# A four-layer hybrid network on one core: layer 0's last convolution, output and attention products arranged anew

## The chip, the cores and the metric

The kernel runs on one core of a Trainium2 chip. The metric is the time of the whole program on the device, in microseconds (us). Engines are named as in the profile: PE (TensorE, matrix products), DVE (VectorE), ACT (ScalarE), POOL (GpSimd), SP (SyncE, which here only issues transfers). Each engine works its own queue in order.

## The reference, cut to what matters

The input is 4 images of 256 channels and 32 x 32 pixels, all in fp32. Four layers follow; the change is in layer 0, a Mamba2 block with a channel attention, and touches the start of layers 1 and 2.

```python
u = layernorm(x over channels) * norm_g + norm_b          # 4 images of 1024 tokens, 256 channels
z, xBC, dt = split(u @ in_w.T)                            # 256, 512, 4 columns
dt = softplus(dt + dt_bias)
xBC = silu(conv1d(xBC, conv_w, 4 taps, causal, per channel) + conv_b)
xs, Bm, Cm = split(xBC)                                   # 256 (4 heads of 64), 128, 128
for t:                                                    # a recurrence over the 1024 tokens
    state = state * exp(dt[t] * A) + dt[t] * xs[t] * Bm[t]
    y[t] = state @ Cm[t]
y = (y + Dp * xs) * silu(z)
y = y * rsqrt(mean(y * y) + 1e-5) * rms_w
out = y @ out_w.T
hdn = relu(mean_over_tokens(out) @ se1_w.T + se1_b)
x = x + out * sigmoid(hdn @ se2_w.T + se2_b)              # one factor per image and channel
```

Layer 1 projects x by three vectors (theta, phi, g), forms one number per token from them, normalises it over all tokens and adds it back, scaled per channel. Layer 2 is softmax attention (Wq, Wk, Wv) and a mixture of 8 experts; layer 3 is an attention over channels and an LSTM over the 1024 tokens.

## The kernel before

The program is written in a tile language: the author issues operations and names tiles, pools give out buffers, and a scheduler at build time decides each engine's order, with semaphores where data or buffers demand a wait. It may move an instruction far ahead of where it is written, unless the code keeps it (`keep_in_program_order`, `issue_after`, `manual_schedule`). On the chip each order is fixed.

**Setup and `_project`** (lines 168 to 314). Weights come by ACT's queue (L177 `w_l0`, L179 `se2`, L181 `wide`: five rows of 256 broadcast to 128 partitions), x by SP's (L239). The tokens go in 8 blocks of 512, two to an image. `load` turns x by PE (L244; the same product gives theta, phi and g of x), ACT copies the rows (L247), DVE copies `of_x` (L248) and takes statistics, POOL makes the reciprocal root, DVE normalises (`un`, L156). `turn` transposes back, `project` makes z, dt (L274) and xBC (L282). After an image's second block `convolve` (L287) makes for each of 4 channel groups one ACT pass (L292), three DVE passes over 1024 columns (L297) and an ACT Silu (L300). After the last block `_decays` (L317) turns all dt into the recurrence's factors, by ACT exp and ln, DVE, and three PE products (L353). The scheduler has put at the head of DVE the scaling of `w_out` by `rms_w` (L199) and that of the LSTM's bias row (L1423), and at the head of ACT the exp of `A_log` (`na`, L347).

**`_scan`** (L359) does the recurrence in 8 tiles of 128 tokens per image. A tile: three transposes and one product on PE (L373, L374); ACT copies `xb` (L376) and makes `au` (L384); PE `pd` (L386), ACT exp (L388), DVE times the mask (`m_h`, L389); three POOL products (`xdt` L392, `y` L398, `xw` L401); PE `py` (L395) and the state's products (L404, L409); on DVE the sums of y (L399, L406, L407), the state (L411, L412) and the gate `zs` (L415); ACT squares (L417).

**`_out`** (L420), once per image: POOL reciprocal roots (L429, L430), DVE diagonals (L437), 16 PE products that scale and turn (L441), ACT copies with sums (`yT`, L445), the pooled sum (L450), its product with `w_out` (L454), mean (L459), product with `w_se1` (L462), ACT relu (`hdn`, L464), product with `se2` (L466), DVE add (`att`, L468), ACT tanh (L469), DVE half (L470), DVE `w_att` = `w_out` times att (L472), six DVE passes that multiply it by theta, phi and g and sum (L476). Then 8 tiles: PE products (L484), DVE adds to `rows` (L487), ACT copy of the three projections (`of_y`, L488). The order as written is recurrence of image b, then output of image b-1; output of the last two images comes after the last recurrence.

**`_layer1`** (L491) is a short chain of DVE and PE on one number per token, ending in `l1_row` (L553). **`_layer2_attention`** (L556) loads `w_l2`, multiplies Wq by Wk (`m_qk`, L590; `b_qk`, L596, L600), and works image by image from there. The LSTM's weights are loaded and scaled (L1415 to L1424) beside the experts of layer 2.

Of the kernel before, what the change touches and what calls it, by code (L numbers as in the profile page):

```python
# [13 lines left out]
ALU = mybir.AluOpType  # L14
# [44 lines left out]
    "norm_g": 2, "norm_b": 2, "conv_w": 16, "conv_b": 4, "rms_w": 2, "se1_b": 1,  # L59
# [64 lines left out]
def _weights(s, name):  # L124
    w = s.wpool.tile([P, C, NW[name]], F32, name=name, tag="w")
    s.nc.scalar.dma_start(w, s.d[name].rearrange("(k p) n -> p k n", p=P))
    return w
# [40 lines left out]
def _layer0_and_1(s):  # L168
# [5 lines left out]
    with ExitStack() as ctx:  # L174
# [5 lines left out]
        wide = keep.tile([P, 5, D], F32, name="wide")  # L180
        nc.scalar.dma_start(  # L181
            wide.rearrange("p i d -> p (i d)"), s.d["wide"].to_broadcast([P, 5 * D])
# [4 lines left out]
            three=wide[:, 2:, :],  # L187
# [10 lines left out]
        for k in range(C):  # L198
            nc.vector.tensor_scalar_mul(  # L199
                v.w_out[:, k, :], v.w_out[:, k, :], s.col["rms_w"][:, k : k + 1]  # L200
            )
        _project(s, v, keep)
        v.dt, v.decay, v.total, v.tail = v.decays
        with ExitStack() as body:
            pools = SimpleNamespace(
                scan=body.enter_context(tc.tile_pool(name="ssm", bufs=2)),
                out=body.enter_context(tc.tile_pool(name="out", bufs=2)),
                ps=body.enter_context(tc.tile_pool(name="ssm_ps", bufs=2, space=PSUM)),
            )
            for b in range(B):  # L210
                _scan(s, v, pools, b)
                if b > 0:
                    _out(s, v, pools, b - 1)
            _out(s, v, pools, B - 1)
# [3 lines left out]
def _project(s, v, keep):  # L218
# [4 lines left out]
    with ExitStack() as ctx:  # L223
# [5 lines left out]
        for k in range(C):  # L229
            nc.vector.tensor_copy(turner[:, k, 3:], s.ident)  # L230
            for j, name in enumerate(("theta_w", "phi_w", "g_w")):
                nc.vector.tensor_copy(turner[:, k, j : j + 1], s.col[name][:, k : k + 1])
        held = {}
# [53 lines left out]
        def convolve(b):  # L287
            for m in range(NXBC):
                x = v.xbc[b][:, m, :]
                acc = pool.tile([P, L], F32, name="acc")  # L290
                tap = s.col["conv_w"][:, m * DCONV : (m + 1) * DCONV]
                nc.scalar.activation(  # L292
                    acc, x[:, off:], AF.Identity,
                    bias=s.col["conv_b"][:, m : m + 1], scale=tap[:, off:],
                )
                for j in range(off):
                    nc.vector.scalar_tensor_tensor(  # L297
                        acc, x[:, j : j + L], tap[:, j : j + 1], acc, ALU.mult, ALU.add
                    )
                nc.scalar.activation(x[:, off:], acc, AF.Silu)  # L300
# [4 lines left out]
        for i in range(NBLK):  # L305
# [7 lines left out]
            if i % BPI == BPI - 1:  # L313
                convolve(i // BPI)


def _decays(s, keep, pool, ps, dtr):  # L317
# [29 lines left out]
    nc.scalar.activation(na, s.row["A_log"], AF.Exp)  # L347
# [11 lines left out]
def _scan(s, v, pools, b):  # L359


    nc, pool, ps = s.nc, pools.scan, pools.ps
    (a, head), xbc, zs = v.decay, v.xbc[b], v.zs[b]
    off = DCONV - 1
    state = pool.tile([P, NH, HD], F32, name="state")
    for c in range(TPI):
        n = b * TPI + c
        t = slice(off + c * P, off + (c + 1) * P)
        bT, cT = xbc[:, 2, t], xbc[:, 3, t]

        ptr = ps.tile([P, 4, P], F32, name="ptr")
        for m in range(3):
            nc.tensor.transpose(ptr[:, m, :], xbc[:, m, t], s.ident)  # L373
        nc.tensor.matmul(ptr[:, 3, :], bT, cT, start=True, stop=True)  # L374
        xb = pool.tile([P, 3, P], F32, name="xb")
        nc.scalar.copy(xb, ptr[:, :3, :])  # L376
        gm = pool.tile([P, P], F32, name="gm")
        nc.vector.tensor_mul(gm, ptr[:, 3, :], s.upper)
        xh = xb[:, :2, :].rearrange("p c (h d) -> p (c h) d", d=HD)


        au = pool.tile([P, NH, P], F32, name="au")
        for h in range(NH):
            nc.scalar.mul(au[:, h, :], s.upper, a[:, n, h : h + 1])  # L384
        pd = ps.tile([P, NH, P], F32, name="pd", bufs=1)
        nc.tensor.matmul(pd, s.lower, au, start=True, stop=True)  # L386
        m_h = pool.tile([P, NH, P], F32, name="m_h")
        nc.scalar.activation(m_h, pd, AF.Exp)  # L388
        nc.vector.tensor_mul(m_h, m_h, _bc(gm, 1, NH))  # L389

        xdt = pool.tile([P, NH, HD], F32, name="xdt")
        nc.gpsimd.tensor_mul(xdt, xh, _bc(v.dt[:, n, :], 2, HD))  # L392
        py = ps.tile([P, NH, HD], F32, name="py", bufs=1)
        for h in range(NH):
            nc.tensor.matmul(py[:, h, :], m_h[:, h, :], xdt[:, h, :], start=True, stop=True)  # L395

        y = pool.tile([P, NH, HD], F32, name="y")
        nc.gpsimd.tensor_mul(y, xh, _bc(s.row["Dp"], 2, HD))  # L398
        nc.vector.tensor_add(y, y, py)  # L399
        xw = pool.tile([P, NH, HD], F32, name="xw")  # L400
        nc.gpsimd.tensor_mul(xw, xh, _bc(v.tail[:, n, :], 2, HD))  # L401
        pst = ps.tile([P, 2, NH, HD], F32, name="pst")
        if c > 0:
            nc.tensor.matmul(pst[:, 0], cT, state, start=True, stop=True)  # L404
            y_in = pool.tile([P, NH, HD], F32, name="y_in")
            nc.vector.tensor_mul(y_in, pst[:, 0], _bc(head[:, n, :], 2, HD))  # L406
            nc.vector.tensor_add(y, y, y_in)  # L407
        if c < TPI - 1:
            nc.tensor.matmul(pst[:, 1], xb[:, 2, :], xw, start=True, stop=True)  # L409
            if c > 0:  # L410
                nc.vector.tensor_mul(state, state, _bc(v.total[:, n, :], 2, HD))  # L411
                nc.vector.tensor_add(state, state, pst[:, 1])  # L412
            else:
                nc.vector.tensor_copy(state, pst[:, 1])
        nc.vector.tensor_mul(zs[:, c, :], zs[:, c, :], y.rearrange("p h d -> p (h d)"))  # L415
        sq = pool.tile([P, D], F32, name="sq")
        nc.scalar.activation(sq, zs[:, c, :], AF.Square, accum_out=v.ss[:, n : n + 1])  # L417


def _out(s, v, pools, b):  # L420


    nc, pool, ps = s.nc, pools.out, pools.ps

# [6 lines left out]
    yT = pool.tile([P, C, L], F32, name="yT", bufs=1)  # L431
# [19 lines left out]
    p = small(P, C)  # L451
    for m in range(C):
        for k in range(C):
            nc.tensor.matmul(  # L454
                p[:, m : m + 1], v.w_out[:, k, bass.ts(m, P)], pooled[:, k : k + 1],
                start=k == 0, stop=k == C - 1,
            )
    mean = pool.tile([P, C], F32, name="mean")
    nc.vector.tensor_scalar_mul(mean, p, 1.0 / L)  # L459
    p = small(NSE, 1)  # L460
    for k in range(C):
        nc.tensor.matmul(p, v.w_se1[:, k, :], mean[:, k : k + 1], start=k == 0, stop=k == C - 1)  # L462
    hdn = pool.tile([NSE, P], F32, name="hdn")
    nc.scalar.activation(hdn, p.to_broadcast([NSE, P]), AF.Relu, bias=s.col["se1_b"][:NSE])  # L464
    p = small(P, D)
    nc.tensor.matmul(p, hdn, v.se2, start=True, stop=True)  # L466
    att = pool.tile([P, D], F32, name="att")
    nc.vector.tensor_add(att, p, v.se2_b)  # L468
    nc.scalar.activation(att, att, AF.Tanh, scale=0.5)  # L469
    nc.vector.tensor_scalar(att, att, 0.5, 0.5, ALU.mult, ALU.add)  # L470
    w = pool.tile([P, C, D + 3], F32, name="w_att")
    nc.vector.tensor_mul(w[:, :, :D], v.w_out, _bc(att, 1, C))  # L472
    for k in range(C):
        for j in range(3):
            junk = pool.tile([P, D], F32, name="junk")
            nc.vector.scalar_tensor_tensor(  # L476
                junk, w[:, k, :D], 1.0, v.three[:, j, :], ALU.mult, ALU.mult,
                accum_out=w[:, k, D + j : D + j + 1],
            )
    for j in range(TPI):  # L480
        n = b * TPI + j
        p = small(P, D + 3)
        for k in range(C):
            nc.tensor.matmul(  # L484
                p, yT[:, k, bass.ts(j, P)], w[:, k, :], start=k == 0, stop=k == C - 1
            )
        nc.vector.tensor_add(s.rows[:, n, :], s.rows[:, n, :], p[:, :D])  # L487
        nc.scalar.copy(v.of_y[:, n, :], p[:, D:])  # L488
# [67 lines left out]
def _layer2_attention(s):  # L556
# [6 lines left out]
    w = _weights(s, "w_l2")  # L563
    wq, wk, wv = (w[:, :, j * D : (j + 1) * D] for j in range(3))
    w_gate = w[:, :, 768:776]
# [5 lines left out]
    with ExitStack() as ctx:  # L571
        keep = ctx.enter_context(tc.tile_pool(name="l2_keep", bufs=1))
# [11 lines left out]

        m_qk = keep.tile([P, C, D], F32, name="m_qk")
        b_qk = keep.tile([P, C], F32, name="b_qk")
        for m in range(C):
            p = slim()
            for k in range(C):
                nc.tensor.matmul(  # L590
# [1240 lines left out]
```

## Time and profile before

| | |
|---|---|
| five runs, median (lowest to highest) | 3439.68 us (3438.15 to 3443.64) |
| the profiled execution: its time, its span | 3440.76 us, 3439.1 us |
| busy: PE, DVE, ACT, POOL | 3119.0, 1840.3, 1099.0, 533.9 us |
| mean granted TensorE clock | 0.986 |
| projection, decays, last convolution | 0 to 150 us |
| recurrence (first `xb` to last square) | 150.15 to 295.5 us |
| output of images 2 and 3 alone | to 337.3 us |
| layer 1 (`l1_row` ready) | to 344.5 us |
| layers 2 and 3 | to 3439.1 us |

Over 3000 of the 3439 us lie in layers 2 and 3, whose code the change leaves as it is but for the moved lines named above. In the profile "busy" is the time in which an engine works; a bracket behind an operation says how long its engine stood idle before it and which operation ended that. Idle time matters only where nothing else sets the pace.

### The profile page before, as it was taken

How to read it: one execution, taken by the hardware profiler on the slowest of the kernel's cores; microseconds unless marked ns; L12 is line 12 of the kernel's file. 1: busy time of each engine (PE TensorE's matmuls, PEld its weight loads, DVE VectorE, ACT ScalarE, POOL GpSimd, SP SyncE). 2: the span in 40 equal slices, each digit the busy share in tenths (PEclk: the TensorE clock that was granted, in tenths of full speed). 3: DMA queues.
4: the chain of work that ended last, by engine and by line, in shares of the span. 5: the costliest groups of instructions: out<-in, count | busy, mean ns of one | idle time of the engine just before them, and what ended most of it. 6: DMA issues, size and time to landing. Idle time of an engine off the chain costs nothing.

```text
span 3439.1 us, 143780 instructions
## 1 busy us (share of the span) xinstructions
PE 3119.0 (91%) x63650; PEld 2503.2 (73%) x63650; DVE 1840.3 (54%) x8205; ACT 1099.0 (32%) x4339; POOL 533.9 (16%) x749
## 2 busy tenths in 40 slices
PE   8797999999999989998998998998998998998887
PEld 5475577688888856777777777777777777777776
DVE  5786644651111144565655565555655665655555
ACT  5763222222222222333332332332332332332222
POOL 2252100124444320001001001001001001001000
PEclk9898899999999999999999999999999999999999
DMA  2000011256666620000000000000000000000000
GB/s 82 1 1 10 1 43 38 102 170 194 193 193 193 189 62 1 4 4 10 4 4 9 4 4 9 5 4 8 6 4 8 6 4 8 6 4 8 6 4 10
DMA packets 49459, 138.94 MB, mean 40 GB/s; under 512 B 4992, under 2 KB 38336, under 8 KB 44224
## 3 DMA queue, kind: packets, MB, share of 16 engines
q0 software_dynamic: 19008, 99.32, 9.3%
q1 hardware_dynamic: 27680, 24.45, 2.2%
q8 instruction: 499, 8.18, 0.9%
q10 hardware_dynamic: 2144, 5.95, 0.5%
q14 instruction: 128, 1.05, 0.1%
HBM read 104.21 MB, written 25.49 MB: 38 GB/s over the span
## 4 chain that ended last, share of the span: by engine, by line
PE 28%; DVE 20%; ACT 10%; issue 5%; DMA 1%; ACTq 0%; POOL 0%; DVEq 0%; SPq 0%
PE pre L1657 16%; DVE col L1668 11%; PE pre L1600 6%; ACT tri L1671 5%; DVE scan L1680 5%; DVE hs L1691 4%; PE p_a L1554 3%; PE p_d L1258 1%; PE p_k L1226 1%; DMA acc<-y,late_rows 1%; ACTq L1671 0%; PE p_d L1266 0%; PE p_w L1246 0%; PE p_w L165 0%; PE p_u L1388 0%
## 5 line engine op out<-in xcount | busy, mean ns | idle before, releaser
L1657 PE MATMUL pre<-w_v,hs 128*4 128x64 f32 x49104 | 872.9, 219 | 210.2 <-DVE hs L1691 199.1
L1657 PEld LDWEIGHTS pre<-w_v,hs 128*4 128x4 f32 x49104 | 684.1, 86 | 399.0 <-DVE hs L1691 397.2
L1600 PE MATMUL pre<-xg,pick 128*128 128x64 f32 x6144 | 903.9, 283 | 0.5 <-DVE xg L1567 0.5
L1600 PEld LDWEIGHTS pre<-xg,pick 128*128 128x128 f32 x6144 | 763.5, 191 | 118.2 <-DVE xg L1567 1.1
L1668 DVE STREAM_TRANSPOSE col<-pre 128x64 f32<-128x64 f32 x2048 | 485.5, 251 | 303.1 <-PE pre L1657 287.9
L1671 ACT ACTIVATE tri<-col 128x16 f32<-128x16 f32 x1024 | 229.5, 224 | 1177.4 <-DVE col L1668 1177.4
L1680 DVE TENSOR_TENSOR_SCAN scan<-tri 128x24 f32<-128x24 f32 x1024 | 217.0, 212 | 361.9 <-ACT tri L1671 361.9
L1562 POOL TENSOR_TENSOR xg<-xg,gate_bias 128x192 f32<-128x192 f32 x127 | 75.0, 591 | 1605.2 <-ACT xg L1561 1605.2
L1152 PE MATMUL ph<-xT,wt 128*128 128x256 f32 x1152 | 256.3, 380 | 1.6 <-issue 0.9
L1162 PE MATMUL po<-wt,hT 128*128 128x256 f32 x1152 | 255.7, 379 | 0.0
L1155 ACT ACTIVATE hT<-ph,wt 128x256 f32<-128x256 f32 x288 | 136.5, 475 | 359.8 <-PE ph L1152 353.3
L1152 PEld LDWEIGHTS ph<-xT,wt 128*128 128x128 f32 x1152 | 207.0, 189 | 43.3 <-ACT hT L1155 5.9
L1162 PEld LDWEIGHTS po<-wt,hT 128*128 128x128 f32 x1152 | 216.0, 190 | 27.8
L1689 DVE STREAM_TRANSPOSE gate<-row 128x64 f32<-128x64 f32 x1024 | 229.1, 224 | 0.7
L1678 ACT ACTIVATE row<-pre 128x64 f32<-128x64 f32 x1024 | 211.3, 206 | 0.6
L1696 DVE SCALAR_TENSOR_TENSOR tri<-hs,scan 128x8 f32<-128x8 f32 x1023 | 182.2, 178 | 36.3 <-DVE hs L1691 1.7
L1132 DVE COPY xT<-p_x 128x512 f32<-128x512 f32 x36 | 24.9, 692 | 210.6 <-PE p_x L1128 210.5
L1173 DVE TENSOR_TENSOR y<-po,wt 128x256 f32<-128x256 f32 x72 | 30.6, 425 | 193.9 <-PE po L1162 184.2
L1554 PE MATMUL p_a<-w_u,u 128*32 128x192 f32 x1792 | 119.3, 338 | 0.0
L732 PE MATMUL p_s<-u,q 128*128 128x512 f32 x256 | 117.9, 600 | 0.0
L766 PE MATMUL p_w<-v,prT 128*128 128x256 f32 x512 | 116.0, 379 | 0.7 <-ACT prT L758 0.7
L766 PEld LDWEIGHTS p_w<-v,prT 128*128 128x128 f32 x512 | 95.5, 190 | 15.5 <-issue 2.9
(2441 smaller groups left out, 3286.4 us busy)
## 6 DMA issues: line engine op xcount, KB each, us to landing
xn<-xn SPq DMA_DIRECT2D x8, 516.0 KB, 3.4
x<-in_x_dram SPq DMA_DIRECT2D x16, 256.0 KB, 3.0
acc<-rows SPq DMA_DIRECT2D x8, 512.0 KB, 2.9
out_dram<-part SPq DMA_DIRECT2D x64, 64.0 KB, 1.7
xn_early<-xn SPq DMA_DIRECT2D x6, 516.0 KB, 5.1
rows<-acc SPq DMA_DIRECT2D x6, 512.0 KB, 8.4
w_l<-in_w_l_dram ACTq DMA_DIRECT2D x1, 1092.0 KB, 9.6
rows<-acc SPq DMA_DIRECT2D x4, 256.0 KB, 4.3
```

What stands on the lines that cost most here:

```text
L766: nc.tensor.matmul(p, prT[:, n, :], images[g // TPI].v[:, n, :], start=n == 0, stop=n == TPI - 1)
L1152: nc.tensor.matmul(ph, w1[:, k, bass.ts(m, P)], xT[:, k, :], start=k == 0, stop=k == C - 1)
L1162: nc.tensor.matmul(po, hT[:, m, bass.ts(j, P)], w2[:, m, :], start=m == 0, stop=m == NHC - 1)
L1554: nc.tensor.matmul(p[32 * j : 32 * (j + 1), :], u3[i * SG // P][:, k, bass.ts(i % (P // SG), 32)], w_u[:, k, j * Q : (j + 1) * Q], start=k ...
L1600: nc.tensor.matmul(p, pick[:, r].rearrange("p j r -> p (j r)"), xg[i][:, v], start=True, stop=t == 0,)
L1657: nc.tensor.matmul(p[32 * j : 32 * j + B, :], hs[:, t - 1, k * B : (k + 1) * B], w_v[:, k, j * Q + v.start : j * Q + v.stop], start=False, ...
L1668: nc.vector.transpose(col[:, g * C : (g + 1) * C, :].rearrange("p n r -> p (n r)"), pre[t % 2][g])
L1671: nc.scalar.activation(z[:, 2:50].rearrange("p (g q) -> p g q", g=2)[:, :, ::3].rearrange("p g (k b) -> p (g k) b", k=C), col[:, :, :B], A ...
L1678: nc.scalar.activation(row, pre[t % 2][2], AF.Tanh)
L1680: nc.vector.tensor_tensor_scan(scan, z[:, 0 : 3 * S], z[:, 26 : 26 + 3 * S], 0.0, ALU.mult, ALU.add)
L1689: nc.vector.transpose(gate.rearrange("p n r -> p (n r)"), row)
L1696: nc.vector.scalar_tensor_tensor(tri[(t + 1) % 2][:, 28:52:3], h, 0.5, cell, ALU.mult, ALU.mult)
```

## The change

- The last image's convolution leaves the projection. It runs in image 0's recurrence, one channel group after every second tile. Silu is written there as h (1 + tanh h) with h half the convolution: weights and bias are halved beforehand on POOL, ACT does tanh, and one more DVE pass per group finishes it.
- `_scan` is called tile by tile. `_out` is parted in `_attention` (up to `w_att`) and one call per output tile. Attention of image b-1 stands after tile 1 of image b's recurrence, its output tiles from tile 4 on, two per tile; in the last recurrence one per tile. The other four tiles of image 2 are placed in the last attention, behind products named by `issue_after`.
- `yT` is written over the x part of `xbc`, which is no longer needed by then.
- `w_out` is scaled after image 0's recurrence, no longer at the head; its transpose and its product with `w_se1` are made once (`out_t`, `w_in`). The product of the pooled sum with `w_out` and the mean go away. att is also made as a column, and theta, phi, g go through `out_t` by four small PE products in place of six DVE passes; `wide` shrinks to two rows.
- `w_l2` is loaded before the recurrence, and `m_qk`, `b_qk` are made at the end of layer 0.
- `na`, the scaling of `w_out` and of the LSTM's weights and bias row are kept where they are written.

```diff
-        wide = keep.tile([P, 5, D], F32, name="wide")
+        wide = keep.tile([P, 2, D], F32, name="wide")
...
-        for k in range(C):
-            nc.vector.tensor_scalar_mul(
-                v.w_out[:, k, :], v.w_out[:, k, :], s.col["rms_w"][:, k : k + 1]
-            )
...
+            s.w_l2 = _weights(s, "w_l2")
+            tc.keep_in_program_order(s.w_load)
...
             for b in range(B):
-                _scan(s, v, pools, b)
-                if b > 0:
-                    _out(s, v, pools, b - 1)
-            _out(s, v, pools, B - 1)
+                for c in range(TPI):
+                    _scan(s, v, pools, b, c)
+                    if b == 0 and c % 2 == 0:
+                        _convolve_last(s, v, pools, conv, c // 2)
+                    if b == 0 and c == TPI - 1:
+                        _out_weights(s, v, pools)
+                    if b > 0 and c == 1:
+                        held = _attention(s, v, pools, b - 1)
+                    if b > 0 and c >= TPI // 2:
+                        n = 1 if b == B - 1 else 2
+                        for j in range(n * (c - TPI // 2), n * (c - TPI // 2 + 1)):
+                            _out(s, v, pools, b - 1, j, held, "p_o")
+            beside = [
+                lambda j=j: _out(s, v, pools, B - 2, j, held, "ptr") for j in range(TPI // 2, TPI)
+            ]
+            last = _attention(s, v, pools, B - 1, beside)
+            for j in range(TPI):
+                _out(s, v, pools, B - 1, j, last, "ptr")
+            _query_weights(s, pools.ps)
...
-            if i % BPI == BPI - 1:
+            if i % BPI == BPI - 1 and i + 1 < NBLK:
                 convolve(i // BPI)
...
+def _convolve_last(s, v, pools, conv, m):
...
+        nc.gpsimd.tensor_scalar_mul(v.half_w, s.col["conv_w"], 0.5)
+        nc.gpsimd.tensor_scalar_mul(v.half_b, s.col["conv_b"], 0.5)
+    acc = _convolution(s, v, conv, B - 1, m, v.half_w, v.half_b)
+    dst = v.xbc[B - 1][:, m, DCONV - 1 :]
+    nc.scalar.activation(dst, acc, AF.Tanh)
+    nc.vector.scalar_tensor_tensor(dst, dst, 1.0, acc, ALU.add, ALU.mult)
...
-    nc.scalar.activation(na, s.row["A_log"], AF.Exp)
+    tc.keep_in_program_order(nc.scalar.activation(na, s.row["A_log"], AF.Exp))
...
+def _out_weights(s, v, pools):
...
+    for m in range(C):
+        p = ps.tile([P, W], F32, name="p_o")
+        for k in range(C):
+            nc.tensor.transpose(p[:, bass.ts(k, P)], v.w_out[:, k, bass.ts(m, P)], s.ident)
+        nc.scalar.copy(v.out_t[:, m, :], p[:, :D])
+    p = ps.tile([P, W], F32, name="p_o")
+    for m in range(C):
+        for k in range(C):
+            nc.tensor.matmul(
+                p[:, bass.ts(m, NSE)], v.out_t[:, k, bass.ts(m, P)], v.w_se1[:, k, :],
+                start=k == 0, stop=k == C - 1,
+            )
+    nc.scalar.copy(v.w_in.rearrange("p m n -> p (m n)"), p[:, : C * NSE])
...
+def _attention(s, v, pools, b, beside=()):
...
+    def fill(product):
+        if beside:
+            with s.tc.issue_after(product.ins):
+                beside.pop(0)()
...
+    p = small(NSE, 1)
+    for k in range(C):
+        mm = nc.tensor.matmul(
+            p, v.w_in[:, k, :], pooled[:, k : k + 1], start=k == 0, stop=k == C - 1
+        )
+    fill(mm)
...
+    p = small(P, D + C)
+    nc.tensor.matmul(p[:, :D], hdn, v.se2, start=True, stop=True)
+    for k in range(C):
+        mm = nc.tensor.matmul(
+            p[:, D + k : D + k + 1], v.se2[:, bass.ts(k, P)], hdn[:, :1], start=True, stop=True
+        )
+    fill(mm)
+    fill(mm)
...
+    mine = pool.tile([P, C, 3], F32, name="mine")
+    nc.vector.tensor_mul(mine, v.three, _bc(att[:, D:], 2, 3))
+    p = small(P, C * 3)
     for m in range(C):
         for k in range(C):
+            mm = nc.tensor.matmul(
+                p[:, 3 * m : 3 * (m + 1)], v.out_t[:, k, bass.ts(m, P)], mine[:, k, :],
                 start=k == 0, stop=k == C - 1,
             )
+    fill(mm)
...
-            junk = pool.tile([P, D], F32, name="junk")
-            nc.vector.scalar_tensor_tensor(
-                junk, w[:, k, :D], 1.0, v.three[:, j, :], ALU.mult, ALU.mult,
-                accum_out=w[:, k, D + j : D + j + 1],
-            )
...
+def _query_weights(s, ps):
...
-        nc.vector.tensor_scalar_mul(io, io, 0.5)
+        s.tc.keep_in_program_order(nc.vector.tensor_scalar_mul(io, io, 0.5))
```

`_query_weights` holds the lines of `m_qk` and `b_qk` that stood in `_layer2_attention`; `_convolution` holds those of `convolve` up to the Silu.

## The prediction

> **What bounds the kernel now.** I read four views: the busy time by stage, the timeline of four places, the rows of single operations, and the waits of each stage. The chain that ended last is followed back only to 1215 us and says nothing of layer 0, so the stages are read one by one. First the busy time by stage: length, busy time of the five engines, granted TensorE clock, DMA share, GB/s.
>
> ```profile
> core 0: us, PE busy (x) PEld busy (x) DVE busy (x) ACT busy (x) POOL busy (x), PEclk, DMA share, GB/s
> 125.00:150.00 25.00, 10.65 (x32) 6.09 (x30) 18.26 (x25) 18.83 (x23) 0.00 (x0) 0.73 0.00 0
> 150.00:187.40 37.40, 34.41 (x182) 25.15 (x182) 28.63 (x68) 31.21 (x94) 21.88 (x33) 0.91 0.01 2
> 187.40:295.20 107.80, 100.67 (x591) 78.52 (x590) 91.75 (x243) 65.38 (x206) 49.61 (x69) 1.00 0.00 1
> 295.20:337.30 42.10, 29.02 (x124) 21.96 (x124) 16.35 (x59) 7.77 (x32) 2.20 (x4) 0.76 0.00 0
> 337.30:351.00 13.70, 7.64 (x27) 6.37 (x28) 6.61 (x27) 0.74 (x2) 3.29 (x13) 0.65 0.17 59
> ```
>
> The rows are: decays and last convolution; image 0 of the recurrence; images 1 to 3 with the output of images 0 and 1 between them; the output of images 2 and 3 alone; layer 1 and the start of layer 2. In the third row PE is 93% busy and sets the pace. In the first, fourth and fifth no engine is near full: chains and in-order queues set them, and the change works there. Now the timeline (start, length, engine, line, and in brackets the idle time before and who ended it):
>
> ```profile
> 11.39 0.62 DVE L199 TENSOR_SCALAR w_l<-w_l,cols 128x256 f32<-128x256 f32 x2 [4.10 <-DMA w_l<-in_w_l_dram]
> ...
> 12.14 5.04 PE L244 MATMUL p_x<-turner,x 128*128 128x131 f32 x20 [2.81 <-DVE of_x L248]
> ...
> 16.97 1.38 DVE L156 TENSOR_SCALAR un<-rows,mv,rstd 128x256 f32<-128x256 f32 x4 [0.75 <-POOL rstd L150]
> ```
>
> ```profile
> 149.02 1.06 ACT L300 ACTIVATE xbc<-acc 128x1024 f32<-128x1024 f32 x1 [2.84 <-DVE acc L297]
> 150.15 0.48 ACT L376 COPY xb<-ptr 128x384 f32<-128x384 f32 x1
> ```
>
> ```profile
> 320.61 0.16 DVE L450 TENSOR_REDUCE pooled<-part 128x2 f32<-128x4 f32 x1 [4.18 <-ACT yT L445]
> ...
> 336.66 0.42 DVE L487 TENSOR_TENSOR rows<-rows,p_o 128x256 f32<-128x256 f32 x1 [0.46 <-PE p_o L484]
> ...
> 347.37 0.16 DVE L600 COPY b_qk<-p_w 128x1 f32<-128x1 f32 x1 [1.57 <-PE p_w L596]
> ...
> 349.93 0.16 DVE L600 COPY b_qk<-p_w 128x1 f32<-128x1 f32 x1 [1.52 <-PE p_w L596]
> ```
>
> At the start DVE stands at L199 until the weights land, and PE behind it. The first `xb` of the recurrence was ready (transposes at 141.27) but stood behind the last Silu. `b_qk` blocks DVE twice ahead of layer 2's statistics. Last, rows of operations (shortest/median/longest ns):
>
> ```profile
> L297 DVE SCALAR_TENSOR_TENSOR acc<-xbc,cols,acc x48: 1253/1280/1286, 46.6 to 147.6; 128x1024 f32<-128x1024 f32 x48
> ```
>
> ```profile
> L406 DVE TENSOR_TENSOR y_in<-pst,head x28: 408/414/425, 156.3 to 293.5; 128x256 f32<-128x256 f32 x28
> L407 DVE TENSOR_TENSOR y<-y,y_in x28: 410/418/832, 162.8 to 294.0; 128x256 f32<-128x256 f32 x28
> ```
>
> The products with two SBUF inputs (L407; likewise L389, L411, L415) are stretched by up to 0.45 us at times; those that read PSUM (L406) never. POOL's own products in the recurrence stretch likewise, 0.61 to 1.1 us. The convolution passes (L297) have two SBUF inputs too, but ran while POOL made none of these products. After the change they run beside them.
>
> **Step by step.** The order of the changed kernel's instructions on each engine is fixed when it is built, and is read there. Times are in the profiled execution: 3440.76 us, 1.66 more than its span and 1.1 above the median 3439.68.
>
> *Start: -3.5.* L199, L1423 (0.43) and the first `na` leave the heads of DVE and ACT. PE's third product waited to 12.14 for the copy behind L199; ACT's copies (the first at 8.49, 0.2 sooner without `na`) now release it at about 8.9: -3.2, and the third copy comes at 9.7, not 13.42. Block 1 of x lands at 11.2 (issued 2.2, 9.0 to landing), so its first copy is at about 11.8, not 15.32: -3.5. PE is 72.66 of 80 us busy from 20 to 100 and hands this on. Bounds: 0 to -4.1 (the whole wait). `wide` is 384 KB smaller in a stretch where the DMA is 93% or more busy; counted at nothing.
>
> *Decays and image 0: +4.* Without the convolution, from the last dtr at 125.9: exp ends 128.4, ln 130.5, one table load and `na` 132.0; on DVE reciprocal and three products end 132.4, `a` 132.7 (before 137.33, four convolution passes stood between). Head, total and tail took 137.45 to 141.22, of which 2.5 were a table load and a convolution pass: now to about 134.3; the weight load's issue adds 0.38 on ACT and its 776 KB meet an idle DMA (share 0.00). Transposes 0.9, first `xb` at 135.6: 14.5 sooner. Three table loads of 1.28 are gone, among this.
> But image 0 now carries 16 passes (12 and 4 that finish the tanh form). Spaced as now (four in 4.86) that is 19.5; ACT's 9.2 and PE stay below. DVE: 28.6 + 19.5 = 48.1. From 150 to 187 the two-input products ran longer than their medians (means 781, 526, 485 and 562 ns against 684, 418, 438 and 419), 3.4 us on some 13; the same quarter on the convolution is 5.1. Of DVE's idle 8.8 I keep 2. Sum 55: from 136.1 to 191.1, against 187.4: +4. Bounds: no collisions and no idle, 184.2 (-3.2); all of POOL's 24 products of 0.61 charged to DVE on top of 48.1, 198.8 (+11.4).
>
> *Images 1 to 3: +5.5.* PE gets image 2's small products (about what L454, L462 and L466 take now: 1.05 + 0.36 + 0.70), four output tiles of 0.93, and the folded weights (four transposes at 0.13, eight loads at 0.12): 7.3. DVE loses 12 passes of L476 for images 0 and 1 (4.2 at a spacing of 0.35); PE waited 7.4 for `m_h` here, and I take a quarter back. Bounds +2 to +12.
>
> *Output alone: -18.* Before, 42.1. After, from the last square Z: rstd and power 2.1 (two POOL products no longer between), first diagonal 0.3, 16 products 4.1, copy 0.8, sum 0.3 (Z+7.6); product 0.4, hidden 0.5, second product beside the first filled tile 1.6, att 0.7, tanh 0.5 (Z+11.2); DVE adds the second filled tile ahead of L549, then half, `mine` and four products 2.0, copy 0.3, last filled tile and one weight product 1.1 (Z+14.6); 8 tiles at 0.93, last add and copy 0.8: Z+22.8. The first two tiles of L484 took 3.0 together after PE had idled, so 1.2 more: 24. What is late next is PE. Bounds -20 to -10 (all 12 tiles at that slow pace, 1.5, and 1 us at two waits).
> The row: those first tiles ran at about 0.43 us a product, later ones at 0.22. [...]
>
> *Layer 1: +1.* Three of the four weight products and the four for `b_qk` stand on PE before layer 1's first product, and a `b_qk` copy between its DVE steps: 1.35 + 0.5 + 0.2 after the last tile, when DVE is ready at 1.45. Bounds +0.5 to +3.
>
> *Layer 2's start: -2.4.* The two waits of 1.57 and 1.52 and their copies (0.32) leave DVE; about 1 returns as waits for POOL's rstd. Bounds 0 to -3.4. The LSTM scaling (0.69, 0.69, 0.95, 0.43) goes behind later expert tiles, where DVE is 17 of 100 us busy and PE full: 0, bounds -2.4 (its wait at 720) to +1.4 (four copies of 0.35 on ACT).
>
> [...]
>
> Sum: -3.5 + 4 + 5.5 - 18 + 1 - 2.4 = -13.4. 3440.8 - 13.4 = 3427.4, in the runs' median 3426.
>
> **Rivals.**
> 1. *More gain, 3415.* POOL and the convolution don't meet, image 0 ends at 184 (-7 more) and images 1 to 3 grow by 2 (-3.5 more). For: POOL works only 22 of 37 us. Against: the quarter measured on the like products.
> 2. *Given back, 3437.* The deferred convolution stretches image 0 by 11 in place of 4 and images 1 to 3 by 10 in place of 5.5. For: DVE has 48 us of work there before any collision, more than the 37.4 of the stage.
> 3. *Slower, 3451.* The attention of the image before, put into tile 1 of each recurrence, blocks the in-order DVE. Its pooled sum, att and halving each wait for a chain of ACT and PE (Z+7.6 to Z+11.6 above; with the wait for the copies some 8 us). At 8 us in each of three images, 24 come back: 3451. It decides above 6.7 a image. For: "ACT att from DVE att" waits 3.9 once now. Against: in the changed order two to four recurrence products stand between each of these steps, and PE's waits in the stretch are only 7 us now, with the same attention in it.
> 4. *The tail does not fold, 3433.* The four filled tiles delay the chain (their adds stand ahead of L549) and the tail takes 31.
>
> **How the numbers follow.** Chances: forecast 0.50, more gain 0.20, given back 0.17, slower 0.08, tail 0.05. A measurement of this kernel tells about 0.2% (6.9 us) from no change, so faster means under 3432.8 and slower over 3446.6. Of the forecast 0.07 lies in "same", of "given back" 0.03 and of the tail 0.02 in "faster": faster 0.43 + 0.20 + 0.03 + 0.02 = 0.68; same 0.07 + 0.14 + 0.03 = 0.24; slower 0.08. The range reaches from well into "more gain", 3409, to just over "given back", 3439.
>
> **What would show it.** Start: `un` at about 13.3, not 16.97. First `xb` some 18 us sooner than 150.15; the convolution's rows in image 0 over 1.28 us, or not. Rstd of image 0 (now 187.44) at about 188, of image 3 (295.58) near 302, layer 1 at about 326, not 337.3. If image 0 ends far from 188, the collision term fails; if the last output takes over 28 us, the tail term.

## The result, and the profile after

The changed kernel takes 3438.41 us (median of 24 runs, 3432.75 to 3441.13) against 3441.30 for the kernel before (44 runs): ratio 0.9991, 95% interval [0.9986, 0.9997]. That is inside the 0.2% that the prediction called no change; it had forecast 3426. The profiled execution took 3439.51 (span 3437.8, before 3439.1). Timed again later beside the kernel before, the same kernel gave 0.9986 [0.9977, 0.9995].

Nearly every stage still moved. The busy time by stage of the changed kernel, in the columns and the order of the prediction's first fence, with the stages cut at the same events:

```profile
core 0: us, PE busy (x) PEld busy (x) DVE busy (x) ACT busy (x) POOL busy (x), PEclk, DMA share, GB/s
121.50:131.50 10.00, 7.50 (x27) 3.78 (x26) 3.74 (x12) 7.80 (x15) 0.46 (x2) 1.00 0.03 5
131.50:187.60 56.10, 42.69 (x179) 26.61 (x177) 49.21 (x84) 38.42 (x97) 29.29 (x33) 0.85 0.04 14
187.60:314.60 127.00, 112.78 (x652) 90.63 (x650) 91.55 (x233) 68.07 (x222) 48.02 (x70) 0.96 0.00 1
314.60:339.70 25.10, 21.36 (x105) 18.15 (x106) 8.53 (x27) 5.74 (x24) 2.12 (x4) 0.86 0.00 1
339.70:350.20 10.50, 3.95 (x21) 3.20 (x19) 5.79 (x25) 0.44 (x3) 2.28 (x12) 0.67 0.00 0
```

The stage of decays and last convolution (25 us) shrank to 10. Image 0 grew from 37.4 to 56.1, with DVE busy 49.2 of it. The output alone fell from 42.1 to 25.1. The third row took it all back: 127.0 us, where images 1 to 3 took 107.8. Its PE was idle for 14.2 us (7.1 before), and its granted clock fell from 1.00 to 0.96. Most of both comes from two places, the seams where one image of the recurrence follows another. From the timeline at the seam of images 1 and 2:

```profile
225.09 0.29 DVE L421 TENSOR_TENSOR gm<-ptr,upper 128x128 f32<-128x128 f32 x1
225.67 0.58 ACT L431 ACTIVATE m_h<-pd 128x512 f32<-128x512 f32 x1
226.97 0.20 POOL L504 TENSOR_SCALAR rstd<-ss 128x8 f32<-128x8 f32 x1
227.25 1.64 POOL L505 TENSOR_TENSOR rstd<-rstd,power 128x8 f32<-128x8 f32 x1
228.92 1.19 DVE L512 TENSOR_SCALAR diag<-ident,rstd 128x128 f32<-128x128 f32 x2 [3.54 <-POOL rstd L505]
230.03 1.11 DVE L432 TENSOR_TENSOR m_h<-m_h,gm 128x512 f32<-128x512 f32 x1
231.29 1.94 PE L438 MATMUL py<-xdt,m_h 128*128 128x64 f32 x8 [2.80 <-DVE m_h L432]
...
233.02 1.17 PE L447 MATMUL pst<-state,xbc 128*128 128x256 f32 x2
```

ACT had `m_h` ready at 226.25. DVE's next instruction, however, was the first diagonal of image 1's attention (L512), which needs `rstd`; POOL computes that only after image 1's last square, behind three products of the next tile. DVE stood 3.54 us, and the `m_h` product of image 2 came 3.8 us late, behind two diagonals. PE waited 2.80 (and 1.07 shortly before, for POOL's `xw`). Then its products ran at half rate: the eight parts of `py` took 1.94 where they take 1.0 to 1.1, `pst` 1.17 where it takes 0.6. The granted clock in the two stretches of 5 us there:

```profile
227.50:232.50 5.00, 2.20 (x9) 1.40 (x8) 3.15 (x7) 2.05 (x6) 3.10 (x4) 0.80 0.00 0
232.50:237.50 5.00, 5.00 (x23) 4.82 (x23) 1.69 (x4) 1.08 (x4) 0.00 (x0) 0.51 0.00 0
```

The seam of images 2 and 3 repeats it at 273.87 to 282: the same 3.54 and 2.80, and `py` in 1.82.

### The profile page after: what moved, and what is told of

Read it like the earlier page. It is cut to its first block, busy times and chain, and to the rows that moved or that the text cites. A ratio compares the mean times of both kernels' runs of the same rounds, so it can differ in the third digit from the quotient of the medians.

```text
span 3437.8 us, 143830 instructions
## 1 busy us (share of the span) xinstructions
PE 3123.3 (91%) x63678; PEld 2506.5 (73%) x63678; DVE 1834.9 (53%) x8165; ACT 1093.7 (32%) x4343; POOL 540.4 (16%) x754
## 4 chain that ended last, share of the span: by engine, by line
PE 27%; DVE 21%; ACT 10%; issue 5%; DMA 1%; ACTq 0%; POOL 0%; DVEq 0%; SPq 0%
PE pre L1745 15%; DVE col L1756 11%; PE pre L1688 6%; ACT tri L1759 5%; DVE scan L1768 5%; DVE hs L1779 4%; PE p_a L1642 3%; PE p_d L1346 1%; PE p_k L1314 1%; DMA acc<-y,late_rows 1%; ACTq L1759 0%; PE p_w L165 0%; PE p_d L1354 0%; PE p_w L1334 0%; PE p_u L1476 0%
```

## The experiments

**Theory A**: the order on DVE at the seams, and the half rate that follows PE's gap, ate the gain. **Rival B**: images 1 to 3 are simply too full (two output tiles per tile of the recurrence, DVE and POOL slowing each other). In the diffs "..." stands for lines left out. All times are from profiles or from comparisons with the kernel before on the same chip.

### The diagonals behind the first m_h

```diff
+    mul = nc.vector.tensor_mul(m_h, m_h, _bc(gm, 1, NH))
+    if c == 0:
+        v.first = mul
...
+            with s.tc.issue_after(v.first.ins):
                 nc.vector.tensor_scalar_mul(diag[:, j, :], ...)
```

> One order changed: on DVE the attention's eight diagonals are put behind the m_h product of the first tile of the next image, ahead of which they stand in the changed kernel. Theory A (order at the seam): at the seams of images 1|2 and 2|3 DVE stands 3.54 us before a diagonal that waits for rstd, m_h comes 3.8 us late, PE is idle 3.9 us, and the products after it run at about half rate for 5 us in all. Then images 1 to 3 take 115 to 118 us in place of 127.1, layer 1 begins 9 to 12 us sooner, time 3427 to 3430. Rival B (crowding): the stall only shows that PE has too much to do (12 us more busy time) and that DVE and POOL slow each other; then PE loses the same elsewhere and the gain is under 3 us: 3435 to 3439.

Measured: 3426.73 us, ratio 0.9964 [0.9952, 0.9976]. Images 1 to 3 took 118.1. The same seam in its timeline, then its three images:

```profile
224.29 1.15 DVE L432 TENSOR_TENSOR m_h<-m_h,gm 128x512 f32<-128x512 f32 x1 [0.90 <-ACT m_h L431]
226.35 1.00 PE L440 MATMUL py<-xdt,m_h 128*128 128x64 f32 x8
227.26 1.19 DVE L515 TENSOR_SCALAR diag<-ident,rstd 128x128 f32<-128x128 f32 x2 [0.95 <-POOL rstd L507]
```

```profile
185.40:225.00 39.60, 36.06 (x221) 29.07 (x219) 31.59 (x78) 21.66 (x73) 15.41 (x22) 1.00 0.00 1
225.00:267.20 42.20, 39.25 (x231) 31.04 (x231) 32.72 (x82) 25.65 (x85) 18.00 (x26) 1.00 0.00 1
267.20:303.50 36.30, 33.68 (x202) 26.63 (x202) 29.02 (x76) 20.60 (x65) 14.90 (x24) 1.00 0.00 1
```

Nothing but the order on DVE was edited. `m_h` goes ahead, the diagonal still waits for `rstd`, now with nothing urgent behind it, and `py` runs in 1.00 at a clock of 1.00. PE's idle time in the three images falls from 14.2 to 9.1 and its busy time from 112.8 to 109.0: 5.1 of waiting and 3.8 of half rate, together 8.9. Image 1, which has no such seam ahead of it, stayed (39.4 and 39.6); images 2 and 3 lost 4.6 and 4.5 each. Theory A holds; B's bound of 3 us does not. That the time lands at the forecast of 3426 is partly luck: image 0, which the edit does not touch, also ended 2.2 us sooner here (`rstd` at 185.39), and the changed kernel, profiled again below, shows that it varies by such an amount without an edit (185.88).

### One output tile to each tile of the recurrence

```diff
-                    if b > 0 and c >= TPI // 2:
-                        n = 1 if b == B - 1 else 2
...
+                    if b > 1 and c < TPI // 2:
+                        _out(s, v, pools, b - 2, c + TPI // 2, before, "p_o")
+                    if b > 0 and c >= TPI // 2:
+                        _out(s, v, pools, b - 1, c - TPI // 2, held, "p_o")
+                before = held
```

> The output tiles of an image go one to each tile of the recurrence, four in the second half of the next image and four in the first half of the one after it (in place of two to each tile of the second half); attention stays after tile 1. So a tile of output stands at each seam, and on DVE m_h of the next image's first tile stands ahead of the diagonals. Theory A: as with the diagonals behind m_h, images 1 to 3 take 114 to 118 us, time 3426 to 3430, within 3 us of that kernel. Rival B (crowding by two output tiles per tile of the recurrence): 6 us or more beyond that kernel, and the wait for POOL's xw in mid-image (1.79 us at 216) goes too.

Measured: 3429.5, ratio 0.9969 [0.9957, 0.9981]; images 1 to 3 took 121.9, above A's 114 to 118. The seams are cured, by the scheduler's own order, but PE's waits for POOL's `xw` rose from 4.4 to 8.2 us. It gained less than the kernel above where B asked for 6 more. So crowding by two output tiles is not what costs the time at the seams.

### The last convolution back in the projection

```diff
-            if i % BPI == BPI - 1 and i + 1 < NBLK:
+            if i % BPI == BPI - 1:
...
-                    if b == 0 and c % 2 == 0:
-                        _convolve_last(s, v, pools, conv, c // 2)
```

> The last convolution goes back into the projection with its Silu, all else as in the changed kernel. Theory A takes the deferral for a small loss: the recurrence starts at about 146 (150.15 before, less the 4.3 of the start), image 0 takes 37 us again, its rstd comes at 183 and not at 187.6; nothing changes after it, so the time falls by 4 to 5: 3434. Rival C (the deferral pays): image 0's rstd at 191 or later, time 3441 or more.

Measured: 3441.19, ratio 1.000 [0.999, 1.0011]; image 0's `rstd` at 192.13, the side of rival C. Its DVE timeline says why:

```profile
143.45 8.69 DVE L336 SCALAR_TENSOR_TENSOR acc<-xbc,cols,acc 128x1024 f32<-128x1024 f32 x6 [0.84 <-ACT acc L332]
152.06 0.28 DVE L419 TENSOR_TENSOR gm<-ptr,upper 128x128 f32<-128x128 f32 x1
```

With the decays kept early, the scheduler put the last six passes ahead of the first `gm`. They ran beside POOL's products, at 1.45 each where 1.28 was the median in the kernel before. Against the one profile of the changed kernel the deferral is worth 3.4 us in this order (4.6 less the 1.2 that this run started late). The figure is rough: from the last `dtr` to image 0's `rstd` this kernel took 69.5 us, the changed kernel 66.1, and the profiles of other kernels in which image 0 is written alike 64.0 to 68.0. Against the order of the kernel before it is not isolated. This profile also lost some 5 us at 690 us, far from the edit (last section).

### The filled output tiles freed

```diff
-            last = _attention(s, v, pools, B - 1, beside)
+            last = _attention(s, v, pools, B - 1)
+            for f in beside:
+                f()
```

> The four output tiles that fill the last attention's waits go behind it, all else as in the changed kernel. Theory A, by the tail's terms: four tiles of 0.93 come after the chain, some at the slow pace after a PE gap, while the chain is 1 us shorter: the last output takes 28 to 31 us in place of 25, time 3442 to 3444. Rival D (the filled tiles delay the chain as much as they save): 24 to 26 us, time 3437 to 3439.

Measured: 3436.22, ratio 0.9989 [0.998, 0.9998]; the last output took 22.7. Both expectations fell. The scheduler moved all four freed tiles ahead of the products with the diagonals, and PE worked on them until 1.2 us after the last square. The 32 products with the diagonals, in the changed kernel and then in this one:

```profile
317.32 6.38 PE L516 MATMUL p_o<-diag,zs 128*128 128x128 f32 x32 [4.81 <-DVE diag L512]
```

```profile
318.08 3.99 PE L518 MATMUL p_o<-diag,zs 128*128 128x128 f32 x32 [1.42 <-DVE diag L514]
```

After a gap of 4.81 the same products took 6.38 us, after 1.42 they took 3.99. The fill that the change wrote into the attention left the gap ahead of it open.

### Both edits together

The first diff and the fourth, on the changed kernel.

> The diagonals behind the first m_h (as in the kernel that tested the seam), and the four filled output tiles put into the program behind the last attention, which lets two of them run in the gap between the last square and the first diagonal. Theory A (a PE gap halves the rate of the products after it): images 1 to 3 stay at 118 us and the last output at 22 to 23 in place of 25.4, because its first 32 products take 4.0 us and not 6.4: time 3423 to 3426. Rival: the two gains are one gain seen twice, or the shorter tail was chance: 3426 to 3430.

Measured: 3427.08, ratio 0.9966 [0.9954, 0.9978], no better than the first edit alone. The freed tiles ended only 0.5 us after the last square here; PE waited 2.21 us, the products took 5.54, and the last output 25.9. The rival's number came, with slow products behind a gap as in theory A.

### The last convolution over three images

On top of both edits:

```diff
-                    if b == 0 and c % 2 == 0:
-                        _convolve_last(s, v, pools, conv, c // 2)
+                    if (b, c) in turns:    # turns = [(0, 0), (0, 4), (1, 0), (2, 0)]
+                        _convolve_last(s, v, pools, conv, turns.index((b, c)))
```

> On top of the diagonals behind the first m_h and the freed output tiles: the four parts of the last convolution go to the tiles (image 0, tile 0), (0, 4), (1, 0) and (2, 0), in place of all four into image 0. Theory A (image 0 is bound by DVE, the images after it by PE, with 8 to 10 us of idle DVE each): image 0 takes 44 to 47 us in place of 54 to 56, images 1 and 2 grow by 1 to 3 each, time 3415 to 3421. Rival B (DVE passes beside the recurrence always delay m_h): images 1 and 2 grow by 4 or more each, time 3423 to 3428.

Measured: 3424.26, ratio 0.9953 [0.9939, 0.9967]. Image 0 took 46.1 (54.3 in the kernel above), image 1 44.9 (39.4), image 2 40.9 (42.2). Image 0 is bound by DVE, as A says. Image 1 gave 5.5 back, as B says, but image 2 gave nothing; the time is B's. Image 1 carried most of two parts: the one written at (1, 0) and three of the four DVE passes of the one at (2, 0) began between 179 and 225 us, several of them at its two seams.

### Two small parts undone

```diff
+        for k in range(C):    # ahead of the projection, and out of _out_weights
+            nc.vector.tensor_scalar_mul(v.w_out[:, k, :], ...)
...
-        s.tc.keep_in_program_order(nc.vector.tensor_scalar_mul(io, io, 0.5))
+        nc.vector.tensor_scalar_mul(io, io, 0.5)
```

> Two small parts undone, all else as in the changed kernel: the scaling of the output weights stands at the head of DVE's queue again, and the scaling of the LSTM weights where the scheduler puts it. Each is read in its own stage. Theory A, by the comparison of the two traces: the first un comes at 16.5 to 17 in place of 13.9 and the recurrence starts 3.5 to 4.3 later; from 700 to 1150 us the place against the kernel before worsens by 1.9. Time 3440 to 3444. Rival (the stages absorb it): under 2 in all, 3437 to 3440.

Measured: 3439.46, ratio 0.9998 [0.9989, 1.0007]. `un` came at 16.82, 2.9 later than in the changed kernel, and the first `xb` at 135.18, 3.7 later: near the costed 3.5. One profile bounds this loosely, as the first `un` of the other kernels with the changed start lay between 13.8 and 15.6. The place against the changed kernel is 4.6 us late at 402 us and 4.9 at the first LSTM step, so the LSTM scaling is worth 0.3 at most. The 1.9 that I had put on it is something else (below), and the time is the rival's.

### PE kept busy at the seam

```diff
+    if b > 1 and c == 0:
+        p = ps.tile([P, W], F32, name="p_o")
+        for _ in range(3):
+            last = nc.tensor.matmul(p, s.lower, au..., start=True, stop=True)
...
+        with s.tc.issue_after(last.ins):    # the parts of py, behind these products
```

> Three products of 128x512 whose result nobody reads are added on PE behind the first decay product of images 2 and 3, so that PE has no long gap at these seams. m_h stays behind two diagonals. If the gap alone sets the slow rate, the products after the stall run at full rate: eight parts of py in 1.0 to 1.1 us and not 1.8 to 1.9, granted clock 1.00 and not 0.51, while m_h still comes late. If the rate falls for another reason (DVE, PSUM), they stay at 1.8 to 1.9. Time within 3433 to 3439.

Measured, in one run: 3436.61 (one time, no interval). The seam on PE:

```profile
226.92 2.74 PE L433 MATMUL p_o<-au,lower 128*128 128x512 f32 x6
231.91 1.08 PE L445 MATMUL py<-xdt,m_h 128*128 128x64 f32 x8 [2.25 <-DVE m_h L438]
232.82 0.65 PE L459 MATMUL pst<-xw,xb 128*128 128x256 f32 x2
```

`m_h` still comes late and PE still waits (2.23 at the other seam), but the products after it run at full rate. `py` alone would not show it: the profiles with the seams unedited are five (the changed kernel twice, the convolution back, the freed tiles, the two parts undone), and in three of their ten seams `py` ran in 1.08 and the half rate came just behind it. The clock does show it: it was lowered for 3.4 or 6.8 us at all ten, and at neither seam here:

```profile
227.00:238.00 11.00, 7.78 (x40) 5.16 (x38) 6.00 (x18) 4.91 (x16) 5.68 (x8) 1.00 0.01 1
272.00:283.00 11.00, 7.81 (x41) 5.30 (x39) 5.97 (x17) 4.95 (x16) 5.43 (x8) 1.00 0.00 1
```

So at these seams the rate followed PE's idleness, not DVE's late work. (The scheduler also moved the other diagonals together here, so the time itself proves little.)

### Six output tiles held for the last gap

On top of both edits, and with only two output tiles, not four, among the tiles of image 3:

```diff
+            with tc.issue_after(v.py.ins), tc.issue_after(v.pst.ins):
+                for f in beside:    # tiles 2 to 7
+                    f()
             last = _attention(s, v, pools, B - 1)
```

> As the kernel with both edits (diagonals behind the first m_h, filled output tiles freed), but six output tiles of image 2 in place of four are left to the end, and on PE they are put behind the last product of image 3's last tile, so that they run in the gap between the last square and the first diagonal. Theory A (a PE gap of 2.2 us or more there is followed by half rate): image 3 is 1 to 2 us shorter, PE has no gap over 1.5 us before the 32 products, these take 4.0 us and not 5.5, and image 3 with the last output takes 58 to 61 us in place of 63.1; time 3422 to 3425. Rival (the products are slow because DVE adds rows beside them, not because of a gap): they stay at 5.5 us, and the time at 3426 to 3429.

Measured: 3433.25, ratio 0.9974 [0.9965, 0.9983]. The 32 products, with no wait ahead of them, took 3.88: theory A's rate. But the rows of the held tiles stood on DVE behind diagonals that wait for `rstd`, so PE waited 2.05 for a buffer, and image 3 with the output took 62.5 (63.1). The ratio is no better than that of the kernel it was built on (0.9966); its profile lost 5 us far away, at 680 us (below).

### Parts of the convolution in mid-image

On top of the held tiles:

```diff
-            turns = [(0, 0), (0, 4), (1, 0), (2, 0)]
+            turns = [(0, 0), (0, 4), (1, 3), (2, 3)]
```

> As the kernel before it, and the four parts of the last convolution at the tiles (image 0, tile 0), (0, 4), (1, 3) and (2, 3), away from the seams. Theory A (DVE has room in the middle of images 1 and 2): image 0 at 46 as in the other kernel that splits the convolution, images 1 and 2 together at 82 to 84 (81.6 with the whole convolution in image 0, 85.8 with parts at the seams); time 3415 to 3420. Rival (a convolution part costs its 5 us of DVE wherever it runs): images 1 and 2 at 86 or more, time 3421 to 3425.

Measured: 3425.99, ratio 0.9956 [0.9942, 0.9969]. Images 1 and 2 took 81.8 together, image 0 45.3, and the first LSTM step came at 1347.4 (1360.3 in the kernel before). A's stages came, its time didn't: the profile shows the same loss at 680 us.

### The changed kernel again, and the best version

First the changed kernel without an edit:

> The changed kernel itself, once more, beside the kernel before on the same chip. Theory A: the two seams stall as in the first profile, because the order on DVE is fixed: diagonals ahead of m_h, m_h about 3.8 us late at each, images 1 to 3 at 126 to 128 us; time 3437 to 3440, that is 0 to 4 below the kernel before. Where one thing is chance: the rate after the gap of 1.71 us at about 685 us, with the same code in every run, has been full in some profiles and half in others; it may differ from the first profile, by up to 5 us. Rival (the stall at the seams is itself chance): images 1 to 3 at 118 to 122 in this profile.

Measured: 3435.95, ratio 0.9986 [0.9977, 0.9995]. DVE stood 3.54 and PE 2.80 at the seam as before; images 1 to 3 took 125.9. The stall is fixed by the order. The half rate was not quite the same: at the first seam the clock was lowered for 3.4 us and not 6.8, and the first `py` took 1.08, the next one 1.81.

Then both edits with the convolution at the mid-image turns, without the held tiles:

> The diagonals behind the first m_h, the four filled output tiles freed, and the four parts of the last convolution at the tiles (image 0, tile 0), (0, 4), (1, 3) and (2, 3). Image 0 at 45 us, images 1 and 2 together at 82, image 3 with the output at 62 to 64, as the earlier kernels with one of these edits showed. Theory A: 3419 to 3424. Rival (the gains do not add, because the images after take on what image 0 gives up): 3424 to 3428.

Measured: 3422.73, ratio 0.9945 [0.9932, 0.9959], the lowest of all, though its interval overlaps those of the kernels at 0.9953 and 0.9956: images 45.5, 42.0, 39.8, 38.9, output 24.3. In the stages the gains add.

## Why the prediction was wrong, step by step

The sum was -13.4; the profiled execution moved by -1.25. By stage, each against the kernel before ("place" is how much later the same instruction starts):

| step | predicted | measured | from |
|---|---|---|---|
| start | -3.5 | -4.3 | last `dtr` 121.43, was 125.74 |
| decays, image 0 | +4 | +4.4 | `rstd` 187.56, was 187.44 |
| images 1 to 3 | +5.5 | +19.0 | last `rstd` 314.65, was 295.58 |
| output alone | -18 | -16.6 | 25.1, was 41.7 |
| layer 1 | +1 | +0.8 | 8.1, was 7.3 |
| layer 2's start | -2.4 | -2.6 | place at 402 us: +0.7 |
| LSTM scaling | 0 | -0.2 | -1.8 at 730, +1.6 by 1150 |
| rest | 0 | -1.8 | -1.7 of it at 685 us |

**The step that failed is "Images 1 to 3: +5.5", bounds +2 to +12.** It counted PE's work and took a quarter of the waits for `m_h` back. The work was nearly right (+7.3 predicted; +8.4 in the kernel with the seams cured). What it put at nothing, without a reason, was the order at the seams. The kernel before already had it at one of the two, that of images 2 and 3:

```profile
257.84 1.77 DVE L437 TENSOR_SCALAR diag<-ident,rstd 128x128 f32<-128x128 f32 x3 [3.55 <-POOL rstd L430]
...
259.53 0.68 DVE L389 TENSOR_TENSOR m_h<-m_h,gm 128x512 f32<-128x512 f32 x1
...
260.26 1.10 PE L395 MATMUL py<-xdt,m_h 128*128 128x64 f32 x8 [2.02 <-DVE m_h L389]
```

There DVE stood as long, PE 2.02 us, and the clock stayed at 1.00; at the seam of images 1 and 2 a diagonal waited only 0.28 for `rstd`. After the change both seams have the stall, PE stands 2.80 at each, and the half rate follows. Both could be seen ahead: the stall in the trace of the kernel before, and the order of instructions on DVE, which was fixed and shows the diagonals in front of the next image's first `m_h`. The first experiment gave 8.9 of the 13.5 us back, about 2 of them the wait that the kernel before had too. Of the other 4.6, some 1.1 is work. The rest is waiting that the sum had at nothing: PE's waits for POOL's `xw` were 0.8 us in the kernel before and 5.4 with the seams cured, while those for `m_h` fell from 4.2 to 1.0. What lengthens the waits for `xw` was not tested.

Some terms were misread besides. The 7.4 of waiting for `m_h` adds PE's 4.5 over the whole recurrence and 2.9 of its weight loads; in images 1 to 3 PE itself waited 4.2. And the stretching of 3.4 us in image 0 stands on 16.6 us of those operations at their medians, not on 13: a fifth and not a quarter. Layer 1's own terms add up to 0.6, not 1.

Rival 3 named the right place, attention in tile 1 blocking DVE, and the wrong step of it: it priced the chain of pooled sum, att and halving at 8 us an image. That chain did find recurrence products between its steps. The wait sat at its first step, and cost 3.8 us of delay and about 2 of half rate, at two seams and not three.

The clock was weighed on the wrong stage. The prediction priced slow products behind a PE gap in the last output alone (1.2 us, on the first two tiles). There the slow rate did cost 2.4 us, on the 32 diagonal products (6.38 us, against 3.99 with the filled tiles freed) and not on the tiles: the granted clock was 0.50 from 315.9 to 322.7 us and 1.00 from there to the end of the stage. At the seams a gap of 2.80 (after 1.07 of idle shortly before) was enough, at all ten seams in the five profiles, and in the kernel with both edits one of 2.21. The sum held nothing for this.

Image 0's sum was right and its parts were not. Forecast were 53.2 us of DVE work and 2 idle; measured 49.2 and 6.9. The collisions are about 2 us and not 5.1: the convolution's passes took 1305 ns in the mean, hardly over the 1280 of before, while `y` plus `y_in` rose from 526 to 763. PE's waits for `m_h` there rose from 0.3 to 6.0 us; that such waits between the engines are what left DVE idle is likely, not shown.

## What to carry to other kernels

When work is moved to sit right behind the value that it needs, look at what stands behind it in the same in-order queue: here a cheap diagonal, ahead of its value, held DVE for 3.54 us and with it the product that feeds the busiest engine. Look for the same stall in the trace before. Read the new order around each wait that the move creates, not only the instruction counts. And price a gap on PE as the gap plus the slow products that can follow it: here 2.80 us and about 2 at each seam, 4.81 and 2.4 in the last output.

## What the runs showed of the hardware

The half rate does not follow the length of the gap alone. Behind 2.02 (kernel before), 2.05 (held tiles), 2.23 and 2.25 us (PE kept busy) the products ran at full rate, behind 2.21 (both edits) at half. At about 680 us every profile has a gap of 1.70 to 1.73 us on PE ahead of eight transposes, with the same code. In 8 of 14 profiles the products after it ran at full rate; in 3 (the kernel before among them) they lost some 1.8 us, in 3 some 5. The lowered clock lasted 3.4 us in the first three and 10.2 in the others. The kernel with the diagonals moved, and the one with the convolution in mid-image:

```profile
675.07 1.64 PE L165 MATMUL p_w<-ident,xn 128*128 128x128 f32 x8 [1.71 <-DVE xn L156]
...
677.41 1.85 PE L792 MATMUL p_w<-w_l,xnT 128*128 128x8 f32 x16
679.11 2.82 PE L823 MATMUL p_s<-u,q 128*128 128x512 f32 x6
```

```profile
669.11 1.64 PE L165 MATMUL p_w<-ident,xn 128*128 128x128 f32 x8 [1.71 <-DVE xn L156]
...
672.20 3.42 PE L798 MATMUL p_w<-w_l,xnT 128*128 128x8 f32 x16
675.47 5.47 PE L829 MATMUL p_s<-u,q 128*128 128x512 f32 x6
```

The gap is equal, the products take twice as long in the second. So two kernels can differ by up to 5 us here without a change at this place: the 1.7 us that the changed kernel gained at 685, which I first put on the LSTM scaling, is this, and so is what the convolution back, the held tiles and the mid-image convolution lost in their profiles. Whether a kernel loses it in every run was not settled; the changed kernel, the only one profiled twice, ran at full rate both times. The lowered stretches lasted 3.4, 6.8 or 10.2 us; what sets their length, and why equal gaps bring them in some profiles only, no run shows. The steps of the LSTM, whose code no run changed, also took from 2065.6 to 2070.7 us between profiles. Stages compared between two traces told causes apart that the total times could not.
